# Attention layer rebuilt: q, k, v once per position, scores on row groups, weighted sums on column groups, GroupNorm folded into the weights

## Chip, cores, metric

One core of one Trainium2 chip runs the whole program. The metric is device time in microseconds (us), the median of several runs. Engines: PE is TensorE (PEld its weight loads), DVE VectorE, ACT ScalarE, POOL GpSimd, SP the DMA-issuing engine. "Clock" is the share of TensorE's full clock that the chip granted. PSUM is the memory, in banks, into which this kernel's matmuls write. "Dense" are the plain full-size matmuls of the projections.

## The reference, cut to what matters

Four images of 384 channels, 64 x 64 positions, all in fp32, go through two layers. Layer 0 is a Mamba-like scan, which the change leaves alone. Layer 1 is neighbourhood attention, 12 heads of 32 channels, each position looking at the 7 x 7 positions around it:

```python
# layer 1, on x = GroupNorm of layer 0's output, then added to it
qkv = einsum('oc,bchw->bohw', w_qkv, x) + b_qkv
k_pad, v_pad = pad(k, 3, mode='edge'), pad(v, 3, mode='edge')
logits[i] = einsum('bnchw,bnchw->bnhw', q * hd**-0.5, k_pad[..., di:di+H, dj:dj+W]) + rel_bias[i]
attn = softmax(logits, axis=-1)                      # over the 49 offsets
out = einsum('oc,bchw->bohw', w_proj, sum_i attn[i] * v_pad[..., di:di+H, dj:dj+W]) + b_proj
```

## The kernel before: layer 1

An image is 8 stripes of 8 rows, a stripe is 4 blocks of 8 x 16 = 128 positions. A block's queries see a window of 14 x 22 = 308 positions; a bias of -1e30 masks what is not in a position's own 7 x 7. I call four heads of one block a unit: 12 units to a stripe, 96 to an image, 384 in all.

```python
# values: projected anew for each block's 308 window positions, though the block has 128
for c in range(3):                                   # 110 + 110 + 88 positions
    pv = bank(ps, "mm")
    for j in range(NJ):
        nc.tensor.matmul(pv[:KN[c], :C], xw[:, j, KOFF[c]:KOFF[c]+KN[c]], w_qkv[:, j, 2*C:], ...)
    nc.vector.tensor_tensor(v[:KN[c], c, :], pv[:KN[c], :C], vb[:KN[c], :], ALU.add)
# scores: three PSUM banks; q of one head (32 rows) is the weight, k of the window moves
lg = bank(ps_l, "lg")                                # bufs=3
nc.tensor.matmul(lg[:, :NK], q[pr, bl, :, :], k[pr, :, window], start=True, stop=True)
# ... maximum on DVE, exp on ACT, transposes of the probabilities on PE ...
# weighted sum: 128 probabilities are the weight, 32 columns of v move
for hh in range(4):
    for c in range(3):
        nc.tensor.matmul(blk["o"][:, cols], pT, blk["v"][:KN[c], c, cols], start=(c == 0), stop=(c == 2))
```

## Time and profile before

| | before |
|---|---|
| median (4 runs) | 11742.58 us |
| one image, layer 0 | about 1660 us, bound by DVE |
| one image, layer 1, first to last score | 1141 us, PE busy 1136 |
| clock in that stretch | 0.86 |

The clock record knows two values, 1 and 0.5, so a mean of 0.86 is 28% of the time at half. Two points of the profile matter later and are not in the prediction. The first is the chain of waits between the layers (start, length, what), where the statistics of the next image stand on the path ahead of layer 1, and x alone at the start of layer 0:

```profile
1815.05 15.25 DMA xs<-in_x_dram
...
3027.36 4.74 DMA xt<-in_x_dram
```

The second is the first-to-last-score stretch of one image in the windows view (length; busy time and count of PE, PEld, DVE, ACT, POOL; granted clock; DMA), by which all later kernels are compared:

```profile
1857.00:2998.00 1141.00, 1135.73 (x5348) 756.37 (x5344) 425.70 (x1217) 322.24 (x935) 33.97 (x45) 0.86 0.03 8
```

### The profile page before, as it was taken

The page shows a single profiled execution, that of the slowest core. Times are in us where ns is not written, and L with a number is a line of the kernel's source. Part 1 is how long each engine was busy: PE and PEld are TensorE (multiplying, and loading weights), DVE is VectorE, ACT ScalarE, POOL GpSimd, SP SyncE. Part 2 cuts the span into 40 slices and gives each one's busy share as a digit, 9 for nine tenths or more (in the row PEclk, how much of TensorE's full clock was granted, in tenths as well). Part 3 has the DMA queues.
Part 4 walks back from the last instruction along what each step waited for, and adds up shares of the span by engine and source line. Part 5 has one row for each costly group of instructions (what it writes and reads, how often), then busy time and mean ns, then how long its engine had stood idle before and what let it go on. Part 6 is the DMA issues. An engine that isn't in the chain of part 4 may idle for free.

```text
span 11729.2 us, 111537 instructions
## 1 busy us (share of the span) xinstructions
PE 10140.4 (86%) x41480; PEld 6212.9 (53%) x41480; DVE 7735.2 (66%) x10709; ACT 4473.3 (38%) x8626; POOL 4149.5 (35%) x1656
## 2 busy tenths in 40 slices
PE   5888878999878887899987888789997888869999
PEld 2444445666444444566644444456664444446666
DVE  3999994333499999333359999833335999983333
ACT  2545442222344444222244544422224454532222
POOL 2666660000266666000036666500003666650000
PEclk8788778888778786888887878688887787868888
DMA  2111001000001110100011111110001111110000
GB/s 64 33 35 33 31 27 56 12 9 6 29 30 35 32 33 24 56 11 9 6 32 34 34 29 32 30 48 11 9 6 33 34 33 35 28 49 6 11 9 9
DMA packets 179382, 317.31 MB, mean 27 GB/s; under 512 B 33660, under 2 KB 36476, under 8 KB 178196
## 3 DMA queue, kind: packets, MB, share of 16 engines
q1 hardware_dynamic: 178836, 310.17, 8.5%
q8 instruction: 325, 5.32, 0.2%
q14 instruction: 221, 1.81, 0.1%
HBM read 256.84 MB, written 53.57 MB: 26 GB/s over the span
## 4 chain that ended last, share of the span: by engine, by line
PE 53%; DVE 35%; issue 6%; ACT 2%; DMA 2%; POOL 1%; SPq 1%; DVEq 0%; ACTq 0%; POOLq 0%
DVE hs L484 24%; PE pv_ps L700 10%; DVE acc L434 8%; PE mm_ps L639 8%; PE lg_ps L655 5%; PE mm_ps L615 4%; PE pt_ps L680 4%; PE hT_ps L423 4%; PE mm_ps L288 2%; PE mm_ps L728 2%; PE mm_ps L340 2%; PE mm_ps L408 2%; PE mm_ps L601 2%; PE pt_ps L691 2%; PE mm_ps L280 1%
## 5 line engine op out<-in xcount | busy, mean ns | idle before, releaser
L476 POOL TENSOR_TENSOR db<-dtx,B 128x1536 f32<-128x1536 f32 x1024 | 3524.0, 3442 | 2102.7 <-issue 1453.1
L484 DVE TENSOR_TENSOR_SCAN hs<-da_ps,state,db 128x512 f32<-128x512 f32 x3072 | 3745.0, 1266 | 275.7 <-ACT da_ps L94 272.0
L423 PE MATMUL hT_ps<-ident,hs 128*128 128x128 f32 x12288 | 2345.4, 342 | 1223.9 <-DVE acc L434 1059.2
L94 ACT ACTIVATE da_ps<-dt,nega 128x512 f32<-128x512 f32 x3072 | 2113.4, 690 | 2277.6 <-DVE hs L484 2276.7
L423 PEld LDWEIGHTS hT_ps<-ident,hs 128*128 128x128 f32 x12288 | 1781.3, 174 | 2220.6 <-DVE acc L434 1566.8
L434 DVE SCALAR_TENSOR_TENSOR acc<-hT_ps,ct,acc 128x768 f32<-128x768 f32 x1920 | 1882.9, 1003 | 354.4 <-PE hT_ps L423 347.9
L94 ACT ACTIVATE sg<-sg,mx 128x308 f32<-128x308 f32 x1536 | 836.7, 545 | 2217.9 <-DVE mx L661 2217.9
L632 POOL COPY xw<-xp 128x924 f32<-128x924 f32 x128 | 124.3, 971 | 3761.1 <-PE mm_ps L639 3761.1
L661 DVE CUSTOM_DVE_ANT_0 sg<-lg_ps,bias 128x308 f32<-128x308 f32 x1536 | 678.8, 476 | 852.9 <-PE lg_ps L655 852.9
L288 PE MATMUL mm_ps<-xn,w_in 128*128 128x512 f32 x2304 | 1110.8, 619 | 13.8 <-DVE xn L327 13.8
L700 PE MATMUL pv_ps<-v,ta 110*128 110x32 f32 x6144 | 1053.1, 298 | 0.6 <-DVE ta L685 0.5
L700 PEld LDWEIGHTS pv_ps<-v,ta 110*128 110x128 f32 x6144 | 968.5, 222 | 55.7 <-issue 21.1
L639 PE MATMUL mm_ps<-w_qkv,xw 128*110 128x384 f32 (+1 forms) x2304 | 933.4, 540 | 8.7 <-DVE o L734 5.9
L645 DVE TENSOR_TENSOR v<-mm_ps,vb 110x384 f32<-110x384 f32 (+1 forms) x384 | 213.6, 556 | 857.1 <-PE mm_ps L639 852.5
L655 PE MATMUL lg_ps<-k,q 32*128 32x308 f32 x3072 | 767.6, 549 | 0.0
L340 PE MATMUL mm_ps<-xb,diag 128*128 128x512 f32 x1536 | 688.0, 592 | 0.0
L685 DVE COPY ta<-pt_ps 110x512 f32<-110x512 f32 x768 | 516.8, 686 | 255.3 <-PE pt_ps L680 233.6
L288 PEld LDWEIGHTS mm_ps<-xn,w_in 128*128 128x128 f32 x2304 | 430.8, 200 | 430.0 <-issue 412.4
L700 PE MATMUL pv_ps<-v,tb 88*128 88x32 f32 x3072 | 640.9, 293 | 1.7 <-ACT tb L695 1.7
L700 PEld LDWEIGHTS pv_ps<-v,tb 88*128 88x128 f32 x3072 | 545.6, 216 | 169.7 <-issue 150.8
L639 PEld LDWEIGHTS mm_ps<-w_qkv,xw 128*110 128x110 f32 (+1 forms) x2304 | 382.0, 182 | 363.3 <-issue 137.2
L680 PE MATMUL pt_ps<-ident,sg 128*110 128x128 f32 x3072 | 562.2, 337 | 0.0
(123 smaller groups left out, 8895.5 us busy)
## 6 DMA issues: line engine op xcount, KB each, us to landing
B<-brows SPq DMA_DIRECT2D x512, 256.0 KB, 3.3
xs<-in_x_dram SPq DMA_DIRECT2D x32, 768.0 KB, 5.9
xt<-in_x_dram SPq DMA_DIRECT2D x32, 768.0 KB, 5.7
xr<-in_x_dram SPq DMA_DIRECT2D x32, 768.0 KB, 4.7
x<-xr SPq DMA_DIRECT2D x32, 768.0 KB, 5.1
x<-x SPq DMA_DIRECT2D x32, 768.0 KB, 5.9
out_dram<-o SPq DMA_DIRECT2D x96, 256.0 KB, 2.0
bias<-bm SPq DMA_DIRECT2D x4, 1848.0 KB, 12.5
```

The costliest lines, as they stand in the source:

```text
L94: ins = nc.scalar.activation(o, i, func, **kw)
L288: nc.tensor.matmul(pb, w_in[:, j, m * P : (m + 1) * P], xn[:, j, :], start=(j == 0), stop=(j == NJ - 1),)
L340: nc.tensor.matmul(pc, diag[:, d, k, :], xb[:, d, k : k + T], start=(k == 0), stop=(k == KC - 1),)
L423: nc.tensor.transpose(hT[:, d * P : (d + 1) * P], hs[:, d, k * P : (k + 1) * P], ident)
L434: nc.vector.scalar_tensor_tensor(acc[:, k, :], hT[:, :DI], c, acc[:, k, :], ALU.mult, ALU.add)
L476: nc.gpsimd.tensor_tensor(db, h["dtx"][:, ds, :], h["B"][n].unsqueeze(1).broadcast_to([P, NJ, T]), ALU.mult,)
L484: nc.vector.tensor_tensor_scan(hs[:, d, :], da, db[:, k, :], state[:, d, n : n + 1], ALU.mult, ALU.add,)
L639: nc.tensor.matmul(pv[: KN[c], :C], xw[:, j, KOFF[c] : KOFF[c] + KN[c]], w_qkv[:, j, 2 * C :], start=(j == 0), stop=(j == NJ - 1),)
L655: nc.tensor.matmul(lg[:, :NK], blk["q"][m][pr, bl, :, :].rearrange("p r c -> p (r c)"), blk["k"][m][pr, :, bl * CB : bl * CB + CW], start= ...
L661: nc.vector.tensor_tensor_reduce(sg[:, hh, :], lg[:, :NK], bias[:, 4 * m + hh, :], -1.0, BIG, ALU.add, ALU.min, mx[:, hh : hh + 1],)
L680: nc.tensor.transpose(pt[: KN[c], col : col + P], sg[:, 2 * pair + hh, KOFF[c] : KOFF[c] + KN[c]], ident,)
L700: nc.tensor.matmul(blk["o"][:, cols], pT, blk["v"][: KN[c], c, cols], start=(c == 0), stop=(c == 2),)
```

## The change

Its intent: project q, k and v once per position and let GpSimd copy the windows; give the scores four PSUM banks so that four heads start together on four 32-row groups; exchange the operands of the weighted sum, so that 32 columns of v are the weight, 128 probabilities move and four heads lie on four 32-column groups; and fold the normalisation into w_qkv, so that the raw x is projected. The normaliser 1/sum is transposed through PE to fit the new layout. To make room, two tensors of layer 0 (the convolution's diagonals, the output weights) are reloaded for each image.

```diff
-    ps_l ... bufs=3      ps_t ... bufs=3
+    ps_l ... bufs=4      ps_t ... bufs=2
+    # weights scaled by the group's 1/sigma, biases from the shift through tiny matmuls
+    nc.vector.tensor_tensor(qb, times_weights(w_qkv, 0, shift), qkb[:, :NJ], ALU.add)
+    nc.vector.tensor_tensor(bv, times_weights(w_qkv, 2 * C, shift), vvb, ALU.add)
+    nc.vector.tensor_tensor(pb, times_weights(w_pj, 0, bv), pjb, ALU.add)
+    act(w_qkv[:, j, :], w_qkv[:, j, :], AF.Copy, scale=gm[:, j, 1:2])
+    for m in range(3 * NJ):                 # q, k, v of a stripe, two stripes ahead
+        pm = bank(ps, "mm")                 # one bank for all dense work
+        nc.tensor.matmul(pm, w_qkv[:, j, m*P:(m+1)*P], xt[:, j, :], ...)
-    nc.tensor.matmul(pv[:KN[c], :C], xw[:, j, ...], w_qkv[:, j, 2*C:], ...)
+    nc.tensor.transpose(pv[:KN[c], m*P:(m+1)*P], vw[:, m, KOFF[c]:KOFF[c]+KN[c]], ident)
-    for hh in range(4):
-        for c in range(3):
-            nc.tensor.matmul(blk["o"][:, cols], pT, blk["v"][:KN[c], c, cols], ...)
+    for c in range(3):
+        for hh in range(4):
+            nc.tensor.matmul(ov[hh*HD:(hh+1)*HD, k, 0, :], v[:KN[c], c, cols], pT, ...)
+    nc.tensor.transpose(ov[:, k, 1, :], rr, ident)      # 1/sum, 32 times each
     # ... (software pipeline of two units, window copies, statistics of the next image: cut)
```

## The prediction

> **What bounds the kernel now.** I read the strip of tenths first, because the kernel has two layers with different limits and the page's shares average them.
>
> ```profile
> PE   5888878999878887899987888789997888869999
> DVE  3999994333499999333359999833335999983333
> PEclk8788778888778786888887878688887787868888
> ```
>
> The strip repeats four times, once per batch. Where VectorE (DVE) stands at 9 the scan of layer 0 runs, which the change leaves as it is; where PE stands at 8 to 9 and DVE at 3 the attention layer (layer 1) runs. So a gain must come from those four stretches. The windows view sizes the first two of them (first matmul of layer 1 to last output), the columns being length, busy time of each engine, granted clock, DMA:
>
> ```profile
> core 0: us, PE busy (x) PEld busy (x) DVE busy (x) ACT busy (x) POOL busy (x), PEclk, DMA share, GB/s
> 1833.00:3025.00 1192.00, 1176.76 (x5472) 777.86 (x5472) 444.30 (x1254) 326.43 (x944) 35.41 (x48) 0.85 0.04 13
> 4730.00:5930.00 1200.00, 1172.04 (x5493) 777.41 (x5493) 449.82 (x1266) 326.97 (x946) 35.73 (x50) 0.86 0.05 16
> ```
>
> PE is busy 98%, DVE 37%, ACT 27%: layer 1 is bound by TensorE alone, and at a granted clock of 0.85. The chain of waits for such a stretch says the same by line:
>
> ```profile
> by line: PE pv_ps L700 25.5%; PE mm_ps L639 18.5%; PE lg_ps L655 13.6%; PE pt_ps L680 10.5%; PE mm_ps L615 10.0%; PE mm_ps L728 6.1%; PE mm_ps L601 5.2%; PE pt_ps L691 5.0%; PE mm_ps L716 1.7%; DVE q L606 0.9%; DMA xt<-in_x_dram 0.8%; DVE o
> ```
>
> Matmul ends are modelled, so I take costs from starts, in the timeline of PE (start, length, line, count of records; an fp32 matmul leaves two records, a transpose one):
>
> ```profile
> 2564.00 0.61 PE L700 MATMUL pv_ps<-v,ta 110*128 110x32 f32 x4
> 2564.45 0.39 PE L700 MATMUL pv_ps<-v,tb 88*128 88x32 f32 x2
> ...
> 2570.82 0.60 PE L691 MATMUL pt_ps<-ident,sg 128*88 128x128 f32 x4
> 2571.26 0.53 PE L700 MATMUL pv_ps<-v,ta 110*128 110x32 f32 x4
> ...
> 2582.85 0.80 PE L655 MATMUL lg_ps<-k,q 32*128 32x308 f32 x4
> 2583.68 2.73 PE L615 MATMUL mm_ps<-xp,w_qkv 128*128 128x490 f32 x6
> 2586.25 0.93 PE L680 MATMUL pt_ps<-ident,sg 128*110 128x128 f32 x7
> ```
>
> From start to next start: weighted sum (L700) 0.45/4 = 0.11 us per record although only 32 columns move, so its 128-column weight load sets the pace; transpose 0.44/4 = 0.11; dense matmul (2586.25 - 2583.68)/6 = 0.43; two heads' scores (L655, four records) 0.83 together. At half clock the same weighted sum takes 0.21, (2525.73 - 2524.88)/4:
>
> ```profile
> 2524.88 1.04 PE L700 MATMUL pv_ps<-v,ta 110*128 110x32 f32 x4
> 2525.73 0.61 PE L700 MATMUL pv_ps<-v,tb 88*128 88x32 f32 x2
> ```
>
> **What the Trainium skill says.** (1) "TensorE: Matmul & The Clock Gate", Part 3: 32-row tiles run concurrently, four row tiles measured 3.07 times, three column tiles 2.38 times. The trace agrees for rows: 308 columns at 0.43/490 us per column are 0.27 us a record, four in series plus the tail would take about 1.3 us, and two heads finish in 0.80. No row shows column tiles here. (2) The same page, Part 1: the clock has two states, full and half, decided in windows of 3.4 us by PE activity. The clock record agrees (only 1.0 and 0.5; a mean of 0.85 means 30% of the time at half), although PE is 98% busy. Sorting one batch's 3.4 us stretches by their content, I find that those with a quarter or more of dense matmul columns keep the full clock and that score and weighted-sum stretches lose it. (3) "TensorEngine Tiling (Array Packing)", PSUM Bottleneck: after a fourfold gain on TensorE the PSUM copies may become the bound. DVE at 37% now says how far off that is.
>
> **The change part by part.** A unit is four heads of one 8x16 block; there are 12 in a stripe, 96 in a batch. PE time at full clock, us per unit:
>
> Before: scores 2 x 0.83 = 1.66; transposes 12 x 0.11 = 1.32; weighted sums 24 x 0.11 = 2.69; values (L639) 18 x 0.32 a block = 5.8, a third 1.93; q, k and output projections 72 x 0.43 a stripe = 31, a twelfth 2.58; output transposes 0.11. Sum 10.29; 96 of them 988; over 0.85 1162, and 1192 is measured. The account holds to 2.5%.
>
> After:
> - Scores: four banks in place of three, so four heads go out together on four row groups: one group of 0.83. Saves 0.83.
> - Weighted sums: v (32 columns) becomes the weight and the probabilities (128 columns) move; four heads lie on four column groups. Per chunk two passes of 0.11 plus an estimated 0.1 of exposed load, times three: 0.95. Saves 1.7.
> - Values: projected once per position, then turned: 9 transposes a block, 1.0, a third 0.33. Saves 1.6. The recomputation in the windows (308 positions for 128, and 14 rows for 8 of k) goes.
> - q, k, v 54 records a stripe and output 18: 72 x 0.43 again, 2.58. So the dense part only trades k's halo for v.
> - Transposes of probabilities stay 1.32; the transposed 1/sum takes 0.11.
> Sum 6.12, of which 3.54 is not dense.
>
> Other engines per unit. DVE: four biased maxima at 0.40 apart plus tail 1.7, two copies 2 x 0.69, the product into aT about 0.29 (0.558 for 384 columns, less 256 at 1.04 ns), reciprocal 0.2, three v copies of 0.55 per block 0.56: 4.2, with latencies 4.4. ACT: four exponentials 0.55 apart 2.3, tb 0.58, reciprocal copy 0.3, nine evictions of 0.68 a stripe 0.5: 3.7. POOL: 18 small window copies a block; from 0.315 us for 126 elements and 0.971 for 924 an estimate of 0.27 to 0.36 each, 5.3 a block, 1.8 a unit. All below PE, except in units without dense work, where DVE's 4.4 takes over from 3.54.
>
> The dense pieces are given out one per unit: nine units of a stripe carry a q/k/v piece (2.58), three of them an output piece too, three carry none. A stripe: 6 x 6.12 + 3 x 8.70 + 3 x 4.4 = 76. The first has no output piece (68), the last two no q/k/v (3 x 6.12 + 9 x 4.4 = 58). Sum 68 + 5 x 76 + 2 x 58 = 564. All dense pieces and value transposes share one PSUM bank, held 57 of 76 us per stripe (2.58 or 0.33 of matmul plus an eviction of 0.7 to 1.0 each), where before it was 80 of 148; I add 12% for stalls: 632.
>
> Outside the loop: two stripes of q, k, v run before the first score with nothing beside them: 18 x (2.58 + 0.95) = 64, first windows and fill 8, the last units and projection 15. Folding the norm (27 tiny matmul pairs, three scalings) about 8 lies beside the loads; the lead-in stays 28, because the next image's statistics move into the loop while the folding comes in. Layer 1 then takes 632 + 64 + 8 + 15 + 28 = 747 against 28 + 1192 = 1220: 473 saved per batch, 1892 in all. Given back: reloading the convolution diagonals and output weights (2.7 MB) at each layer 0, an estimated 6 us each, 24; and a clock that I put at 0.96 rather than 1, about 20 per batch, 80. 11739 - 1892 + 24 + 80 = about 9950.
>
> **Rivals.**
> 1. Column groups do not overlap (fp32 passes in series). The weighted sums then cost 24 x 0.11 = 2.6 as now. Against it: the row groups do overlap with the same two-pass records. Cost 1.65 in the PE-bound units, about 120 per batch: 10400.
> 2. The clock drops: units without dense work look like the stretches that run at half clock today. For it: 0.85 now. Against it: four tiles fill the array for shorter, so the same work is denser in time. At 0.85 in the new loop, about 90 per batch: 10250.
> 3. The single bank or DVE becomes the wait; 25% stalls instead of 12% give 73 per batch: 10240. With none and a full clock: 9600.
> 4. A later start of layer 0 or POOL's windows arriving late (5.3 us of copies in a slot of some 6): 10 to 60 per batch.
>
> **Range and chances.** Removing the PE work is certain for values (1.6 of 10.29 per unit), likely for scores, probable for column groups. Even rivals 1 and 2 together leave about 10700. I say 9950, 9550 to 10450 in 8 of 10, faster 0.985, same 0.012, slower 0.003.
>
> **What would show it.** Layer 1's windows at about 720 us of loop and ends instead of 1192, with layer 0 at its 1655. The score group of eight records in about 0.8 us; a weighted-sum chunk of eight records in about 0.3 (if 0.9, rival 1). PEclk in layer 1 above 0.9 (if 0.85, rival 2). DVE busy near 450 us per batch as now, hence 60% of a shorter stretch. PE idle ahead of L-lines that use the shared bank shows rival 3. I am wrong if DVE or POOL heads the chain of waits through layer 1.

## The result, and the profile after

| | before | after |
|---|---|---|
| median (4 runs each) | 11742.58 us | 9814.72 us |
| ratio | | 0.8358 (0.8344 to 0.8373) |
| layer 1, first to last score, first image | 1141 us | 618 us |
| clock in it | 0.86 | 0.98 |

A ratio is the mean time of one kernel's fast runs over that of the other's in the same rounds, so it is not quite the ratio of the medians. The forecast of 9950 was 135 us too long, and its range holds the result.

The strip of tenths after (40 slices of the whole span):

```profile
PE   4888887799788788779978788878997888886899
DVE  1999999456599999945659999994565999999356
PEclk9787787799888788789988778878998878886999
```

The stretches where DVE falls off are now some three slices of 245 us an image, not four of 293, and the clock stands at 8 to 9 in them. DVE is at 5 to 6 instead of 3: nearly the same work (389 us busy, 426 before) in about half the time. The windows view of the first image:

```profile
1914.00:2532.00 618.00, 600.56 (x4952) 345.21 (x4956) 388.54 (x1280) 322.09 (x1001) 149.76 (x661) 0.98 0.11 36
```

PE is still busy 97% of it, so TensorE still bounds the layer. The chain of waits through the loop agrees, with DVE lines small:

```profile
by line: PE mm_ps L607 22.4%; PE lg_ps L682 16.3%; PE pt_ps L713 11.2%; PE ov L748 9.0%; PE mm_ps L773 8.7%; PE mm_ps L669 6.2%; PE pt_ps L727 6.0%; DVE sg L698 4.8%; DMA xs<-in_x_dram 4.5%; PE ov L752 2.8%; DVE ta L718 2.7%; issue 2.2%; DV
```

The PE timeline shows both kinds of groups (start, length, line, records):

```profile
2002.65 0.78 PE L682 MATMUL lg_ps<-kw,q 32*128 32x308 f32 x2
2003.36 0.54 PE L669 MATMUL mm_ps<-ident,vw 128*110 128x128 f32 x3
2003.83 0.79 PE L682 MATMUL lg_ps<-kw,q 32*128 32x308 f32 x4
...
2007.08 0.64 PE L748 MATMUL ov<-ta,v 110*32 110x128 f32 x16
2007.54 0.40 PE L748 MATMUL ov<-tb,v 88*32 88x128 f32 x8
2007.87 0.33 PE L752 MATMUL ov<-ident,rrep 128*128 128x128 f32 x1
...
2011.15 0.80 PE L682 MATMUL lg_ps<-kw,q 32*128 32x308 f32 x8
2011.88 1.09 PE L713 MATMUL pt_ps<-ident,sg 128*110 128x128 f32 x8
```

The 24 records of a weighted sum now take 2007.87 - 2007.08 = 0.79 us, against 2.69. Four heads' scores (eight records, at 2011.15) take 0.73 us; but one head alone (two records, at 2002.65) takes 0.71 as well. A group has a price, whatever stands in it. Counting the trace, the 384 units' scores went out in 636 groups: 212 of four heads, 40 of three, 184 of two, 200 of one. The source writes a unit's four scores one after another; the instructions between them are the scheduler's doing, which, as I read it, puts value transposes and dense pieces in when the first score bank comes free.

### The profile page after: what moved, and what is told of

It is laid out like the page before. It is cut to its first block, busy times and chain, and to the rows that moved or that the text cites. A ratio compares the mean times of both kernels' runs of the same rounds, so it can differ in the third digit from the quotient of the medians.

```text
span 9816.2 us, 114437 instructions
## 1 busy us (share of the span) xinstructions
PE 8171.9 (83%) x40544; PEld 4645.3 (47%) x40544; DVE 7514.8 (77%) x10857; ACT 4534.7 (46%) x8990; POOL 4636.1 (47%) x4216
## 4 chain that ended last, share of the span: by engine, by line
DVE 44%; PE 41%; issue 8%; ACT 4%; DMA 2%; POOL 1%; SPq 1%; DVEq 0%; ACTq 0%; POOLq 0%
DVE hs L491 28%; DVE acc L441 10%; PE mm_ps L607 8%; PE hT_ps L430 5%; PE lg_ps L682 4%; PE pt_ps L713 3%; PE mm_ps L295 3%; PE mm_ps L347 3%; PE mm_ps L415 3%; PE mm_ps L773 3%; PE ov L748 2%; PE pt_ps L727 2%; PE mm_ps L669 2%; DVE sg L698 1%; PE mm_ps L287 1%
## 5 line engine op out<-in xcount | busy, mean ns | idle before, releaser
L607 PE MATMUL mm_ps<-x,w_qkv 128*128 128x512 f32 x1728 | 814.1, 608 | 49.9 <-ACT kv L618 30.0
L736 POOL COPY rrep<-rsum 128x128 f32<-128x128 f32 x384 | 113.7, 296 | 1297.9 <-DVE rsum L734 1295.8
L464 PE MATMUL mm_ps<-xc,w_out 128*128 128x512 f32 x1152 | 550.2, 624 | 6.5 <-POOL xc L457 2.9
L638 POOL COPY kw<-kv 128x66 f32<-128x66 f32 (+1 forms) x1152 | 255.1, 272 | 575.8 <-PE lg_ps L682 511.0
L607 PEld LDWEIGHTS mm_ps<-x,w_qkv 128*128 128x128 f32 x1728 | 317.8, 197 | 416.3 <-issue 282.9
L682 PE MATMUL lg_ps<-kw,q 32*128 32x308 f32 x3072 | 509.6, 475 | 0.9 <-POOL kw L638 0.9
L673 DVE COPY v<-mm_ps 110x384 f32<-110x384 f32 (+1 forms) x384 | 212.7, 554 | 292.0 <-PE mm_ps L669 290.4
L713 PE MATMUL pt_ps<-ident,sg 128*110 128x128 f32 x3072 | 434.6, 281 | 0.2
L347 PEld LDWEIGHTS mm_ps<-xb,diag 128*128 128x128 f32 x1536 | 277.5, 189 | 288.5 <-issue 288.5
L713 PEld LDWEIGHTS pt_ps<-ident,sg 128*110 128x110 f32 x3072 | 332.4, 134 | 142.6 <-issue 105.1
```

What stands on the lines that cost most here:

```text
L347: nc.tensor.matmul(pc, diag[:, d, k, :], xb[:, d, k : k + T], start=(k == 0), stop=(k == KC - 1),)
L464: nc.tensor.matmul(po, w_out[:, d, m * P : (m + 1) * P], h["xc"][:, d, :], start=(d == 0), stop=(d == ND - 1),)
L607: nc.tensor.matmul(pm, w_qkv[:, j, m * P : (m + 1) * P], xt[:, j, :], start=(j == 0), stop=(j == NJ - 1),)
L682: nc.tensor.matmul(lg[:, :NK], qs[s][pr, m, bl, :, :].rearrange("p r c -> p (r c)"), kws[s, bl][pr, m, :], start=True, stop=True,)
L713: nc.tensor.transpose(pt[: KN[c], col : col + P], sg[:, 2 * pair + hh, KOFF[c] : KOFF[c] + KN[c]], ident,)
```

## The experiments

"Layer 1" below is the first-to-last-score stretch of the first image; differences are in medians, against the changed kernel's 9814.72 or against the kernel before in the same rounds. The kernel before itself had medians of 11726 to 11743 in the four sets of rounds (0.14%), so differences of 20 or 30 us between kernels of different rounds are rough.

| kernel | median us | ratio to before (95%) | layer 1 us | its clock |
|---|---|---|---|---|
| before | 11742.58 | | 1141 | 0.86 |
| after | 9814.72 | 0.8358 (0.8344 to 0.8373) | 618 | 0.98 |
| before, column groups alone | 10692.54 | 0.9118 (0.9104 to 0.9133) | 889 | 0.99 |
| before, a third of the values | 11524.09 | 0.9832 (0.9809 to 0.9856) | 1127 | 0.77 |
| before, 128 columns of v moved | 11345.96 | 0.9671 (0.9655 to 0.9688) | 1046 | 1.00 |
| after, head by head | 10018.88 | 0.8541 (0.8525 to 0.8557) | 661 | 1.00 |
| after, one column group | 10483.06 | 0.8935 (0.8922 to 0.8948) | 776 | 0.99 |
| after, three score banks | 10029.29 | 0.8549 (0.8534 to 0.8564) | 668 | 0.99 |
| after, values again | 10538.62 | 0.8984 (0.8971 to 0.8997) | 794 | 1.00 |
| after, scores together | 9734.92 | 0.8297 (0.8283 to 0.8311) | 596 | 0.99 |
| after, two banks first | 9749.84 | 0.8310 (0.8298 to 0.8323) | 616 | 0.99 |
| after, x before weights | 9783.13 | 0.8339 (0.8326 to 0.8351) | 617 | 0.99 |
| after, the last three together | 9624.36 | 0.8203 (0.8191 to 0.8215) | 593 | 1.00 |

### 1. The column groups alone, on the kernel before

```diff
-            nc.tensor.matmul(blk["o"][:, cols], pT, blk["v"][:KN[c], c, cols], ...)
+            nc.tensor.matmul(ov[hh*HD:(hh+1)*HD, k, 0, :], blk["v"][:KN[c], c, cols], pT, ...)
+    # with the transposed 1/sum and the product into aT; block_end() and its transposes go
```

> The kernel before with the weighted sum alone turned to column groups (with its reciprocal transposes; the output transposes go). PE work per unit falls by 2.69 - 0.8 + 0.11 - 0.17 = about 1.8 us at full clock, 384 units: 700 us; VectorE, ACT and POOL have room. Theory (tiles fill the array, so the clock does not fall): 700 to 1000 us shorter, the clock of layer 1 at 0.87 or more. Rival (the clock was held by the dense parts alone): clock 0.85 or less, 500 to 700 us shorter.

It came out 1034 us shorter, so just past the upper end of the 700 to 1000, and the clock at 0.99:

```profile
1857.00:2746.00 889.00, 862.75 (x5350) 446.57 (x5349) 429.12 (x1341) 326.53 (x994) 60.88 (x140) 0.99 0.03 11
```

One part of the change brings more than half of its gain (1034 of 1928), and more than its 700 us of saved PE work: the clock rose with it. That the dense matmuls alone held the clock, as my prediction had it, falls here. That their work is the same as before would not be enough, because it lies closer together in a shorter layer; but of the 221 stretches of 3.4 us at full clock in which no dense matmul moved a column, 206 kept it, against 37 of 162 in the kernel before.

### 2. How the weighted sum is spread over the array

Two kernels, both from the changed one. Head by head on the four column groups:

```diff
-                for c in range(3):
-                    for hh in range(4):
+                for hh in range(4):
+                    for c in range(3):
```

> The changed kernel, but the 12 matmuls of a weighted sum are issued head by head instead of chunk by chunk, so that six records in a row belong to one column group. Theory (four column groups at once are what cut the sum from 2.7 to 0.79 us per unit): nearly serial again, 2.2 to 2.7 us per unit, 500 to 700 us longer in all if the clock of layer 1 stays near 0.98, more if it falls. Rival (the gain comes from the narrow weights, 32 columns loaded instead of 128): the sum stays near 0.8 us and the time within 1% of the changed kernel.

And, head by head, all in one column group:

```diff
-                            ov[hh * HD : (hh + 1) * HD, k, 0, :], v[: KN[c], c, cols], pT,
+                            ov[:HD, k, 0, :], v[: KN[c], c, cols], pT,
```

> The changed kernel with all four heads' weighted sums written to one and the same column group, head by head (wrong result on purpose): v is still the narrow weight and the probabilities still move, but nothing can lie beside anything. Theory (concurrency of column groups is the whole gain of the weighted sum): 24 records of 0.11 = 2.6 us per unit against 0.79 in the changed kernel and 1.52 head by head on four groups; 400 to 650 us longer than the changed kernel. Rival (exchanging weight and moving operand already gave part of it): 1.5 us per unit or less. Clock theory (array cells in use per time): with a quarter of the columns in use for 2.6 us the clock of layer 1 falls from 0.98 to 0.85 to 0.93; rival: it stays at 0.98.

One column group: 24 records take 2.75 us (2006.29 to 2009.04 below) and the kernel is 668 us longer than the changed one, as the theory of concurrency says (just over its 400 to 650). Exchanging the operands gains nothing by itself in PE time; the old form took 2.69.

```profile
2006.29 0.62 PE L749 MATMUL ov<-ta,v 110*32 110x128 f32 x4
2006.75 0.38 PE L749 MATMUL ov<-tb,v 88*32 88x128 f32 x2
...
2008.73 0.38 PE L749 MATMUL ov<-tb,v 88*32 88x128 f32 x2
2009.04 0.33 PE L753 MATMUL ov<-ident,rrep 128*128 128x128 f32 x1
```

Head by head on four groups missed my 2.2 to 2.7 us: the sum takes 1.52, and the kernel is only 204 us longer instead of 500 to 700.

```profile
2006.19 0.65 PE L748 MATMUL ov<-ta,v 110*32 110x128 f32 x6
...
2007.71 0.33 PE L752 MATMUL ov<-ident,rrep 128*128 128x128 f32 x1
```

The single records behind these lines suggest why. The second head's first record starts 0.25 us after the first head's, not 0.6, when three of the first head's six have started: here a matmul for a free column group started while two or three earlier ones for a busy group were still in line (one weighted sum was looked at in this way). About two heads overlap instead of four (2.75/1.52 = 1.8). So chunk by chunk, with neighbouring instructions on different groups, is the order to write.

The clock expectation for the one group (0.85 to 0.93) missed too: 0.99. A quarter of the array's columns in use for 2.75 us of each unit does not pull the clock down.

### 3. What holds the clock

I had taken dense matmuls for it. First a third of the value matmuls on the kernel before (the note in its expectation that begins "1966 us" is a slip of arithmetic, corrected there to 492):

```diff
-                    for j in range(NJ):
+                    for j in range(1):
                         nc.tensor.matmul(pv[: KN[c], :C], xw[:, j, ...], w_qkv[:, j, 2 * C :],
```

> The kernel before with one of the three accumulated matmuls of each value chunk (wrong result on purpose): 12 records of 0.32 us fewer in each of 512 blocks over the four images, 1966 us... per image 128 blocks would be wrong; there are 32 blocks per stripe row set, 8 stripes x 4 blocks = 32 per image, 128 in all: 12 x 0.32 x 128 = 492 us at full clock. Plain count: 492/0.85 = about 580 us shorter at an unchanged clock. Theory of the clock (dense columns are what keeps it up): layer 1's clock falls below 0.85, to 0.78 to 0.82, and the gain is only 150 to 400 us. Rival (the clock does not depend on them): clock 0.85, 490 to 600 us shorter.

The clock fell to 0.77 (0.80 in the other three images) and the kernel got 202 us shorter rather than 580. More than half of what the removed work was worth went into a slower clock. This agrees with the dense theory, which experiment 1 and the one column group refute; so I looked for a quantity that fits all. I cut each image's layer 1 into the clock's 3.4 us stretches and counted, from the starts of the records, in what share of a stretch any columns were moving through the array, at 0.84 ns a column (512 columns in 0.43 us, dense). Then, for stretches at full clock, whether the next one was at full clock too:

```
columns moving, share of the stretch   before: stretches, kept   after: stretches, kept
0.30 to 0.40                           114, 0                    1, 0
0.40 to 0.45                            25, 8                    7, 1
0.45 to 0.50                            87, 83                   6, 6
0.50 to 0.60                            63, 61                   5, 5
0.60 and over                          670, 670                674, 674
```

(A repeat of the count agrees from 0.45 up. Below that it hangs on the 0.84: the repeat put 69 and 68 of the old kernel's stretches into the two lowest rows, of which 0 and 6 kept the clock.)

It does not matter what moves, nor how many of the array's columns its weights fill. In the one-column-group kernel 76 stretches used only 0.2 to 0.3 of the cells while columns moved 0.90 of the time, and all 76 kept the clock; in the kernel before, of 123 stretches with the same use of cells but columns moving 0.37 of the time, none did. But 0.45 is not the rule. In the column groups alone, of 16 stretches with columns moving 0.53 to 0.56 of the time 15 lost the clock, and with a third of the values 28 of 49 between 0.45 and 0.50 did. A recount over all 13 traces fits better if each moment is weighed by the share of the array's 128 rows into which columns move (110 rows for a piece of weighted sum, 32 for a score of one head), and then one bound serves both layers:

```
columns moving, weighed by rows   layer 1: stretches, kept   outside it: stretches, kept
under 0.35                          311, 0                    1737, 0
0.35 to 0.40                        101, 51                    637, 154
0.40 and over                     10346, 10338               13589, 13588
```

The best single bound misplaces 28 of the 10758 stretches of layer 1 with this weight and 95 without it. This is a fit after the fact; no run was made to test the rows.

The old weighted sum is what moved little: it loads 128 columns of weights for 0.11 us and moves 32 columns in 0.027.

If movement is what counts, by either measure, more work at the same pace must make the kernel before faster. Its weighted sum can move 128 columns of v instead of 32 for nothing, because the weight load sets the pace:

```diff
-    nc.tensor.matmul(blk["o"][:, cols], pT, blk["v"][: KN[c], c, cols],
+    wide = slice(cols.start, cols.start + P)     # the surplus is overwritten by later heads
+    nc.tensor.matmul(blk["o"][:, wide], pT, blk["v"][: KN[c], c, wide],
```

> The kernel before with more work: each weighted-sum matmul moves 128 columns of v instead of 32 (the surplus is overwritten or unread, the result stays right). Its 128-column weight load paces a record at 0.11 us either way, so no record gets shorter at a given clock, and as many records remain. Theory (the clock is kept by the share of time in which columns stream through the array, about 0.45 of each 3.4 us being enough): the clock of layer 1 rises from 0.86 to 0.97 or more and the kernel gets 400 to 600 us shorter, layer 1 falling from 1141 us to about 1000. Rival (the clock follows the dense work, or the cells in use for useful sums): clock 0.86, time within 1% of the kernel before, or longer.

```profile
1857.00:2900.00 1043.00, 1029.02 (x5326) 649.34 (x5324) 417.42 (x1212) 319.94 (x929) 44.26 (x75) 1.00 0.03 9
```

(The window ends 4 us before the last score, hence 1046 in the table.) The clock of layer 1 is 1.00 in all four images, and the kernel is 385 us shorter with a correct result and not one matmul fewer (400 to 600 was expected: direction and clock right, the size a little under). The rival, no change, is out: more movement alone brings the clock back.

### 4. The fourth score bank

```diff
-            ps_l ... bufs=4      ps_t ... bufs=2
+            ps_l ... bufs=3      ps_t ... bufs=3
```

> The changed kernel with three score banks and three transpose banks, as before. The instruction order on TensorE is almost the same (209 groups of four heads instead of 212). Theory (the fourth bank lets four heads start together): where four stand together the fourth waits for VectorE to read the first, about 0.8 us later, so 150 to 300 us longer in all. Rival (VectorE reads them in time anyway, the bank is not needed): within 0.5%.

215 us longer, within the 150 to 300. The timeline shows the wait, ahead of the fourth head (two records) and released by DVE's maximum of the first:

```profile
2002.62 0.79 PE L682 MATMUL lg_ps<-kw,q 32*128 32x308 f32 x6
2003.98 0.78 PE L682 MATMUL lg_ps<-kw,q 32*128 32x308 f32 x2 [0.57 <-DVE mx L698]
```

### 5. The values computed again

```diff
                     pv = bank(ps, "mm")
+                    for j in range(NJ):
+                        nc.tensor.matmul(pv[: KN[c], :C], vw[:, j, ...], w_qkv[:, j, 2 * C :], ...)
                     for m in range(NJ):
                         nc.tensor.transpose(pv[: KN[c], m * P : (m + 1) * P], ...
```

> The changed kernel, which also computes the values of each block's window anew as the kernel before did (18 records of about 0.32 us per block, then overwritten by the transposes; same result). Theory (TensorE bounds the loop, so each dense record costs its length): 18 x 0.32 x 128 = 740 us longer at a clock that stays at 0.98 or more; 600 to 850 allowed for the shared bank and the units that wait for VectorE. Rival (the loop is held by VectorE or the shared bank): under 350 us, or over 1000.

724 us longer at a clock of 1.00: 128 blocks at 5.7 us, the full length of 18 records. Nothing of it was hidden, so TensorE does bound the loop, and not DVE. The added matmuls also hold the shared bank, so this run does not rule that out; the waits of PE in the changed kernel's loop do (total us, times, longest). Of 622 us it stands 3.9 for the shared bank (DVE v) and 0.2 for POOL's windows:

```profile
PE pt_ps L727 <- DVE ta L718: 13.4, 25, 1.7
PE mm_ps L669 <- DVE v L673: 3.9, 11, 0.8
PE lg_ps L682 <- POOL kw L638: 0.2, 1, 0.2
```

### 6. What is left in the changed kernel

All scores of a unit behind the dense piece and the value transposes written before them, by an ordering dependence without a wait:

```diff
+                    if hh == 0:
+                        after_late(ins)      # order after the last matmul of each piece so far
```

> The changed kernel with the scores of a unit kept behind the dense piece and the value transposes that were written before them, so that all 384 groups have four heads (in the changed kernel 212 of 636 have). Theory (each extra group costs its 0.71 us, as one group does whatever its heads): 252 groups fewer, 180 us, less some waiting for the shared bank: 80 to 180 us shorter. Rival (the split groups only fill time in which TensorE would wait for the shared bank): within 0.5% or longer.

All 384 units now have groups of four, and the kernel is 80 us shorter (9734.92): the lower edge of the 80 to 180. 252 groups at 0.71 us would be 179; about half came back, so the split groups did fill some waiting, but not all of it.

The pieces ahead of the loop in two banks:

```diff
-                    pm = bank(ps, "mm")
+                    pm = bank(ps_t, "pt") if spare else bank(ps, "mm")
```

> The changed kernel with the 18 q, k, v pieces ahead of the loop spread over the two transpose banks. Theory: the 17 waits of 0.68 to 0.78 us go, 12 us per image, 48 in all. Rival: the evictions follow one another anyway and less than 15 us are won.

65 us shorter by the medians, 48 expected, and clear of the interval. The first tile of x ahead of the reloads:

```diff
+            first = prepared(0, cur, None)
+            next(first)                      # issues the load of x
             nc.sync.dma_start(diag..., diag_d)
             nc.sync.dma_start(w_out, ...)
```

> The changed kernel with the first tile of x loaded ahead of the two reloads at each start of layer 0. Theory: the first dense matmul of layer 0 comes 7 us earlier for each of the four images as in the kernel before, 20 to 30 us in all. Rival: the reloads then delay the convolution or another load, under 10 us.

32 us shorter by the medians, of the expected size, but its interval overlaps the changed kernel's, so the time alone does not settle it. The chain of waits does show the load of x back at its old length (4.88 us, where the changed kernel has 10.69):

```profile
2545.11 4.88 DMA xt<-in_x_dram
```

All three:

> The changed kernel with all scores together, the q, k, v pieces ahead of the loop spread over the two transpose banks in place of one, and the image's first tile loaded ahead of the reloaded weights at each start of layer 0. Theory: scores 80 to 180 us, the 17 waits of about 0.7 us before the loop times four 47 us, the reloads up to 30 us: 150 to 250 us shorter than the changed kernel, 9560 to 9670. Rival (each wait only moves to another place): under 80 us shorter.

9624.36 us, 190 shorter than the changed kernel and 0.8203 of the kernel before: the best version found, with a correct result. 80 + 65 + 32 = 177 is close to it.

## Why the prediction was right, step by step

**What bounds layer 1, and the sum.** Right. Per image, from the last statistic of layer 0 to the last output, I had 747 us; the trace has 26 before the first piece (1821.70 to 1847.70), 66 ahead of the loop, 622 in it and 15 after it: 729. Before it was 1220.

**Weighted sums.** 0.95 us forecast, 0.79 measured; one column group shows that the concurrency is all of it. Rival 1 is out.

**Values.** 1.6 us a unit, or 614 in all, forecast; putting the matmuls back costs 724, the transposes staying. Less these transposes, which I had at 0.33 us a unit or 127 in all, it is about 600.

**Scores.** Off by size. "Four heads go out together on four row groups: one group of 0.83" holds for 212 of 384 units. A group takes 0.73, but with 636 groups the average unit has 1.27 (488 us of group time over 384 units), not 0.83. The fourth bank alone is worth 215 us.

**Loop and stalls.** 632 forecast, 622 measured (1914 to 2536). That they agree so well is luck in part. The scores cost 0.44 us a unit more than I had, some 42 us an image; the 12% for stalls, 68 us, stood for the shared bank (rival 3), for which PE hardly waits, and took them up. Units without a dense piece take 3.73 us, the distance of two groups of four scores at the end of an image, where I had 4.4 from DVE's sum:

```profile
2524.37 0.80 PE L682 MATMUL lg_ps<-kw,q 32*128 32x308 f32 x8
...
2528.10 0.80 PE L682 MATMUL lg_ps<-kw,q 32*128 32x308 f32 x8
```

**The clock: the step with the wrong reason.** I charged 80 us for a clock of 0.96 and, as rival 2, feared more, because I read that "those with a quarter or more of dense matmul columns keep the full clock". What counts is the movement of columns of any kind, as far as the counts above tell. The clock of layer 1 is 0.98 to 1.00, rival 2 is out, the charge was not due, and the rise is a gain of its own: 385 us on the kernel before, where nothing else changed. I had divided the old work by 0.85 and so priced it in the difference, without seeing that the old weighted sum was its cause. That my account of the old kernel closed to 2.5% was luck as well: dividing 988 by 0.85 charges the clock with 174 us an image, and the run that restored it won 96 (385 in all). The rest were waits and gaps that I had not counted.

**Lead-in.** 28 forecast, 26 measured, but for other reasons than I gave. The statistics of the next image left the path, as I said; the folding did not lie "beside the loads" but on the path, 3 x 4.0 us of tiny matmuls one after another:

```profile
1825.81 8.66 DMA w_qkv<-in_qkv_wT_dram
...
1834.92 3.98 PE mm_ps L578 x18
...
1839.14 4.01 PE mm_ps L578 x18
...
1843.40 4.00 PE mm_ps L578 x18
```

**Reloads.** 6 us an image forecast. From the last output to layer 0's first dense matmul it is 33.3 us (2550.6 to 2583.9) where it was 25.8: 7.5, with the load of x at 10.69 us behind them:

```profile
2553.65 10.69 DMA xt<-in_x_dram
```

**The account closed.** 1220 - 729 = 491 in the first image, 1964 for four, less 30 of reloads: 1934, and 1928 is measured. By experiments: 1034 for the column groups (clock included), 724 for the values, 215 for the bank, 1973 together. Each was taken in other surroundings, and the 724 leaves the new transposes out, so that the sum comes so close is partly chance. No run took the folding of the normalisation out alone, and what is left of the stalls inside the loop was not taken apart further.

## What to carry to other kernels

When the array is busy all the time and the granted clock is still below one, ask how long columns actually move, and into how many rows: a matmul with a 128-column weight load and few moving columns costs twice, once in its own time and once in the clock of its neighbours. Exchange the operands so that the narrow one is the weight, and write neighbouring instructions to different 32-wide groups, as many as there are banks free. Count the groups that really left together, because a group of one head costs what a group of four does.

## What the Trainium skill lacked or had wrong

- "TensorE: Matmul & The Clock Gate", Part 4, has it that the full clock does not engage for transposes. Here, in fp32, they count like other matmuls: of some 50 stretches of the changed kernel in which everything but transposes moved only 0.2 to 0.3 of the time, 0.67 with them, all but one kept the full clock.
- The same page, Part 1, names an activity window but no amount. With moving columns weighed by the rows that they enter, the full clock was kept, over all 13 traces, in 0 of 2048 stretches under 0.35 and in 23926 of 23935 from 0.40 up. A PE that is busy all the time (1136 of 1141 us) with weight loads and few moving columns loses it; how many of the array's columns are in use did not count.
- The same page, Part 3, gives 2.38 for three column tiles. Four column groups in fp32 measured 2.75/0.79 = 3.5, and 1.8 (2.75/1.52) if the instructions of one group follow one another. The page does not say that the order of issue decides.
